# GpSimd computes the factors of a batch's second norm right behind the power of its first

## The chip, the cores and the metric

The kernel runs on one core of a Trainium2 chip, as one launch. The metric is the device time in microseconds (us), lower is better. A comparison uses the median of several runs. The profile is of one further execution, taken by the hardware profiler.

## The reference

One decoder layer over `x` of 16 batches x 256 tokens x 256 features, fp32 throughout. Three sublayers, each added to its input and followed by a layer norm without gain or bias:

```
x = norm(x + recurrent(x))            # projection, causal convolution over 4 tokens, silu,
                                      # a scan over 16 states, projection
x = norm(x + xattn(ctx, latents=x))   # x normed AGAIN inside (rsqrt of its variance, gain, bias),
                                      # q from x, keys/values from 77 context rows and x, 8 heads of 128
x = norm(x + experts(x))              # top 2 of 8 experts, 512 tokens each at most
```

What matters here is the second line: the output of the first norm is normed once more inside the attention. Its mean is 0, so this second norm is a multiplication of each token by one factor, `rsqrt(var * r * r + eps)`, where `var` and `r` are the first norm's variance and reciprocal root.

## The kernel before

**Tiling and stages.** Tokens lie on 128 partitions, so a batch is two tiles of 128 tokens. The main loop runs over 128 heads, 16 batches of 8. For head (b, h) TensorE (PE in the profile) makes keys and queries (`head_kq`: `pk` L609, `pq` L614), then the output of an earlier head (`po` L660), scores (`s` L624) and the transposes of an earlier head's probabilities (`pa`, `pb` L646). ScalarE (ACT) does the exponentials, VectorE (DVE) the maxima (`nm` L626), the reciprocal of the sum (`rs` L632), the division (`p` L634) and a copy of the transposes (`ptt` L648). After the attention the experts follow.

**What is woven in.** Between the heads of batch b the steps that prepare batch b + 1 and finish batch b - 1 are issued, by a table that is written by hand (`steps`, `mid_steps`, `late_steps`: at a given head, ahead of its scores, or behind them). The steps of interest, for a batch nb = b + 1 that is even (b odd):

- head 1: `rec_out(nb)`: the first norm of batch nb. DVE takes mean and variance (L144 to L147), GpSimd (POOL) the power `ra` = (var + eps) ** -0.5 (L136), DVE writes the normed `xs` (L151).
- behind head 1: `scatter_second(b - 3)`, four indirect DMAs that GpSimd issues (L990): rows of two earlier batches go to the experts' lists `xg`. They are held behind `normed[b + 1]`.
- head 2: `project_pairs(b - 1, 0)`: the attention's output projection of batch b - 1, its first three groups of products on PE (`pw`, L750). For it GpSimd adds the residual and the output's bias, `xb = xs + bo` (L743, two instructions), also held behind `normed[b + 1]`.
- head 2: `prep_norm(nb)`: GpSimd computes the factors of the second norm in `again`: `uz` (L159), `u2z` (L161), `u3z` (L163) and the power `rlz` (L136), each on 128x2 values. DVE multiplies `xs` by them: `zl`, two instructions (L522).
- behind head 2: `project_sums(b - 1, 1)`: DVE makes sums of the attention's output for the rest of the projection: `ot` (L729) and `osum` (L730). PE's second part of `pw` at head 3 reads them. Then DVE adds the first part of the projection into `xb` (L764).

For an odd nb, `rec_out(nb)` stands at head 3 of batch b and `prep_norm(nb)` at head 0 of the next batch; there `settle` (factors `uo` to `rlo`, GpSimd's product `o`, L807, and its store to the output on SyncE's queue, SP) and `xb` of another batch stand between the two on GpSimd. Batch 0's are ahead of the loop.

**What sets the order.** Each engine executes its instructions in order. The order on an engine comes from the tile framework's scheduler, which starts from the order in which the program issues instructions and moves them by its own estimates of when each is ready; `tc.issue_after(i)` keeps an instruction from being placed ahead of instruction `i`. `normed[b]` names that instruction: the last power that was recorded (`powers[-1]`) when batch b's first norm was issued.

Of the kernel before, what the change touches and what calls it, by code (L numbers as in the profile page):

```python
# [38 lines left out]
def decoder_layer(  # L39
# [94 lines left out]
    def rsqrt(v, n, rows, name):  # L134
        r = small.tile([P, n], F32, tag="r", name=f"r{name}")
        powers.append(G.tensor_tensor(r[:rows], v[:rows], nhalf[:rows, 0:n], ALU.pow))  # L136
        return r

    def layernorm(dst, src, n, rows, name, behind=None):

        mv = small.tile([P, n, 2], F32, tag="mv", name=f"mv{name}")
        for i in range(n):
            st = small.tile([P, 6], F32, tag="st", name=f"st{name}_{i}")
            V.bn_stats(st[:rows], src[:rows, i, :])  # L144
            V.bn_aggr(mv[:rows, i, :], st[:rows])
        v = small.tile([P, n], F32, tag="v", name=f"v{name}")
        V.tensor_scalar(v[:rows], mv[:rows, :, 1], EPS, None, ALU.add)  # L147
        r = rsqrt(v, n, rows, name)
        for i in range(n):
            with tc.issue_after(behind.ins) if behind is not None else nullcontext():  # L150
                V.tensor_scalar(  # L151
                    dst[:rows, i, 0:D], src[:rows, i, :], mv[:rows, i, 0:1], r[:rows, i : i + 1], ALU.subtract, ALU.mult
                )
        return mv, r

    def again(mv, r, name):

        u = small.tile([P, 2], F32, tag="u", name=f"u{name}")
        G.tensor_tensor(u, mv[:, :, 1], r, ALU.mult)  # L159
        u2 = small.tile([P, 2], F32, tag="u2", name=f"u2{name}")  # L160
        G.tensor_tensor(u2, u, r, ALU.mult)  # L161
        u3 = small.tile([P, 2], F32, tag="u3", name=f"u3{name}")
        G.tensor_scalar(u3, u2, EPS, 1.0, ALU.add, ALU.mult)  # L163
        return rsqrt(u3, 2, P, f"l{name}")
# [40 lines left out]
    def load_x(b):  # L205
        xts[b] = aw.tile([P, 2, D], F32, tag="xt", bufs=3, name=f"xt{b}")
        nc.sync.dma_start(xts[b], x_in[b * S : (b + 1) * S, :].rearrange("(i p) d -> p i d", p=P))
# [116 lines left out]
    sums, yss, xs, stats = {}, {}, {}, {}  # L324
# [90 lines left out]
        for b, r in zip(members, rows):  # L415
            yss[b] = ys[r, :], outw[r, :]

    ysums, normed = {}, {}

    def rec_add(b, n):  # L420

# [12 lines left out]
    def rec_out(b):  # L434

        xs[b] = xpool.tile([P, 2, DX], F32, tag="xs", name=f"xs{b}")
        stats[b] = layernorm(xs[b], ysums.pop(b), 2, P, f"a{b}")
        normed[b] = powers[-1]
        if b + 2 < B:
            load_x(b + 2)  # L440
# [70 lines left out]

    def prep_norm(b):

        r2 = again(*stats.pop(b), f"z{b}")
        zl = b1.tile([P, 2, D], F32, tag="zl", name=f"zl{b}")
        for i in range(2):
            if turned is None:
                V.tensor_scalar(zl[:, i, :], xs[b][:, i, 0:D], r2[:, i : i + 1], None, ALU.mult)
                continue

            with tc.issue_after(turned.ins):
                V.tensor_scalar(zl[:, i, :], xs[b][:, i, 0:D], r2[:, i : i + 1], None, ALU.mult)  # L522
        zs[b] = zl
# [497 lines left out]
    for b in range(B):  # L1021
# [26 lines left out]
        if new_pair:  # L1048
# [3 lines left out]
            elif nb % 4 == 0:  # L1052
                at(b, 0, rec_state, nb, nb + 3)
                amid(b, 0, rec_scan, nb)
            at(b, 1, rec_add, nb, PB)
            at(b, 1, rec_out, nb)
            at(b, 2, prep_norm, nb)
            at(b, 3, rec_out, nb + 1)
            at(b, 3, prep_keys, nb)
            at(b, 3, prep_sums, nb)  # L1060
# [3 lines left out]
        elif b == 0:  # L1064
            for h in range(2):
                at(0, h, rec_in, 0, 2 * h, 1)
                at(0, h, rec_in, 0, 2 * h + 1, 1)
            at(0, 2, load_xT, 1)
            at(0, 2, rec_state, 1, 1)
            amid(0, 2, rec_scan, 1)  # L1070
            at(0, 3, rec_add, 1, 1)
            at(0, 3, rec_out, 1)
            at(0, 4, prep_norm, 1)
            at(0, 4, prep_keys, 1)
            at(0, 4, prep_sums, 1)
            for n, h in enumerate((5, 6, 7)):
                at(0, h, prep_values, 1, n, False)
                behind(0, h, prep_values, 1, n, True)
            for h in range(NCT - FIRST_CTX):
                behind(0, h, context, FIRST_CTX + h, False)  # L1080
        elif nb < B:
            at(b, 0, prep_norm, nb)
            at(b, 0, prep_keys, nb)
            at(b, 0, prep_sums, nb)
            for n, h in enumerate((1, 4, 6)):
                at(b, h, prep_values, nb, n, False)
                behind(b, h, prep_values, nb, n, True)
# [378 lines left out]
```

## Time and profile before

| | us |
|---|---|
| runs | 1169.77, 1172.89, 1169.11 |
| median | 1169.77 |
| the profiled execution | 1171.0 |
| its span, first to last instruction | 1169.3 |
| PE busy | 1135.1 |
| DVE busy | 782.1 |
| ACT busy | 499.0 |
| POOL busy | 316.1 |

Times in rows of the profile are microseconds from the span's start. Busy PE time is that of pipelined matmuls, so neighbouring groups overlap by some 0.2 us. A row that merges several instructions says how many (x4) and gives the time from the first one's start to the last one's end. Tile names have their buffer numbers left out: `ra` is the power of a batch's first norm, `rlz` that of its second, `rb` that of the norm behind the attention, `rlo` that of the last `again`. `A <- B` in a wait means that A's engine stood idle until B was done.

### The profile page before, as it was taken

What the parts mean: (1) busy time and instruction counts of PE and PEld (TensorE: products, weight loads), DVE (VectorE), ACT (ScalarE), POOL (GpSimd) and SP (SyncE); (2) the same over time, 40 slices, a digit from 0 to 9 for tenths busy, and PEclk for the clock granted to TensorE, in tenths of its full rate; (3) what the DMA queues carried; (4) which work ended last, traced back from release to release, by engine and by line L of the source; (5) the groups of instructions that cost most, each with busy time, mean ns of one, the idle gap of its engine ahead of it and who ended that gap; (6) DMA issues with size and microseconds to landing.
All of it is one profiled execution on the core that took longest, in us unless ns stands there. A gap on an engine that the chain in (4) does not pass through costs nothing. (4 is left out here: it accounts for less than half of the span.)

```text
span 1169.3 us, 16020 instructions
## 1 busy us (share of the span) xinstructions
PE 1135.1 (97%) x5380; PEld 821.0 (70%) x5380; DVE 782.1 (67%) x2144; ACT 499.0 (43%) x1315; POOL 316.1 (27%) x565
## 2 busy tenths in 40 slices
PE   7999999999999999999999999999999999999996
PEld 3465676767787777677777777777777778876664
DVE  6655877676657776777567757865567555665666
ACT  3344444453444344444444444444444444523331
POOL 2201241114210530242015302340142014144455
PEclk9999999999999999999999999999999999999998
DMA  8741010001000110010000100000001000046652
GB/s 276 206 128 39 20 38 18 11 28 58 19 12 10 54 36 12 28 40 19 12 10 27 37 11 10 18 19 12 10 17 46 20 10 15 21 159 138 181 160 90
DMA packets 47417, 60.63 MB, mean 52 GB/s; under 512 B 7957, under 2 KB 37374, under 8 KB 47336
## 3 DMA queue, kind: packets, MB, share of 16 engines
q1 hardware_dynamic: 39686, 50.18, 14.1%
q0 software_dynamic: 6048, 9.22, 3.3%
q8 instruction: 42, 0.69, 0.2%
q10 hardware_dynamic: 1602, 0.23, 0.1%
q14 instruction: 39, 0.32, 0.1%
HBM read 36.33 MB, written 30.78 MB: 57 GB/s over the span
## 5 line engine op out<-in xcount | busy, mean ns | idle before, releaser
L660 PE MATMUL po<-ptt,v 128*128 128x256 f32 (+1 forms) x768 | 189.2, 381 | 1.6 <-DVE rs L632 1.6
L660 PEld LDWEIGHTS po<-ptt,v 128*128 128x128 f32 (+1 forms) x768 | 142.0, 190 | 51.7 <-issue 34.4
L609 PE MATMUL pk<-kvt,wkv_s 128*128 128x333 f32 x512 | 165.4, 444 | 0.0
L624 PE MATMUL s<-kt,qt 128*128 128x333 f32 x512 | 164.5, 443 | 0.0
L626 DVE TENSOR_REDUCE nm<-s 128x2 f32<-128x666 f32 x128 | 108.3, 846 | 72.1 <-PE s L624 68.1
L630 ACT ACTIVATE p<-s,nm 128x333 f32<-128x333 f32 x256 | 135.7, 536 | 44.5 <-DVE nm L626 44.2
L614 PE MATMUL pq<-kvt,wq_s 128*128 128x256 f32 x512 | 131.2, 378 | 0.0
L609 PEld LDWEIGHTS pk<-kvt,wkv_s 128*128 128x128 f32 x512 | 91.1, 191 | 45.6 <-issue 22.9
L668 ACT ACTIVATE ot<-po,bkv_s 128x256 f32<-128x256 f32 x128 | 60.9, 476 | 140.3 <-PE po L660 135.7
L624 PEld LDWEIGHTS s<-kt,qt 128*128 128x128 f32 x512 | 96.3, 188 | 31.6 <-issue 1.3
L614 PEld LDWEIGHTS pq<-kvt,wq_s 128*128 128x128 f32 x512 | 96.7, 189 | 30.8 <-issue 1.0
L649 ACT COPY ptt<-pb 77x256 f32<-77x256 f32 x128 | 47.3, 369 | 164.1 <-PE pb L646 161.0
L634 DVE TENSOR_SCALAR p<-p,rs 128x333 f32<-128x333 f32 x256 | 98.5, 421 | 3.3
L990 POOL DMA_INDIRECT xg<-xs,sidx x64 | 66.1, 1032 | 98.3 <-ACT ot L668 38.9
L648 DVE COPY ptt<-pa 128x512 f32<-128x512 f32 x128 | 87.3, 682 | 0.7 <-PE pa L646 0.7
L646 PEld LDWEIGHTS pa<-ident,p 128*128 128x128 f32 x512 | 63.9, 141 | 29.3
L611 ACT ACTIVATE kt<-pk,bkv_s 128x333 f32<-128x333 f32 x128 | 69.1, 540 | 28.2 <-PE pk L609 21.7
L646 PE MATMUL pa<-ident,p 128*128 128x128 f32 x512 | 76.8, 273 | 0.0
L351 DVE SCALAR_TENSOR_TENSOR cv<-hp,cw,cv 128x512 f32<-128x512 f32 (+1 forms) x108 | 74.1, 692 | 1.6
L616 ACT ACTIVATE qt<-pq,bqs 128x256 f32<-128x256 f32 x128 | 61.1, 478 | 20.2 <-PE pq L614 15.3
L336 PE MATMUL ph<-xT,inw 128*128 128x512 f32 (+1 forms) x144 | 63.1, 567 | 5.5 <-DMA inw<-in_in_wT 4.4
L1275 PE MATMUL pf<-w,it 128*128 128x256 f32 x272 | 61.3, 381 | 2.0 <-ACT ye L1285 1.7
(264 smaller groups left out, 1764.6 us busy)
## 6 DMA issues: line engine op xcount, KB each, us to landing
v<-vc SPq DMA_DIRECT2D x16, 308.0 KB
xg<-zero SPq DMA_DIRECT2D x34, 131.0 KB
xe<-xg SPq DMA_DIRECT2D x8, 524.0 KB
xt<-in_x_in SPq DMA_DIRECT2D x16, 256.0 KB
out<-o SPq DMA_DIRECT2D x16, 256.0 KB
w<-in_w1T SPq DMA_DIRECT2D x8, 512.0 KB
w<-in_w2T SPq DMA_DIRECT2D x8, 512.0 KB
oe<-ye SPq DMA_DIRECT2D x15, 256.0 KB
```

Source lines behind the costliest of these rows:

```text
L351: conv = V.scalar_tensor_tensor(cv, hp[:, :, k : k + S], cw[:, c, k : k + 1], cv, ALU.mult, ALU.add)
L609: T.matmul(pk[:, 0:J], lhsT=wkv_s[:, k, f], rhs=kvt[:, k, :], start=(k == 0), stop=(k == DC - 1))
L611: A.activation(kt, pk[:, 0:J], AF.Identity, bias=bkv_s[:, h : h + 1])
L614: T.matmul(pq[:, 0:S], lhsT=wq_s[:, k, f], rhs=kvt[:, k, 0:S], start=(k == 0), stop=(k == DC - 1))
L624: T.matmul(s[:, ic, 0:J], lhsT=qt[:, ic * P : (ic + 1) * P], rhs=kt, start=True, stop=True)
L626: V.tensor_reduce(nm, s[:, :, 0:J], AX.X, ALU.max, negate=True)
L630: A.activation(p[:, ic, :], s[:, ic, 0:J], AF.Exp, bias=nm[:, ic : ic + 1], accum_out=sm[:, ic : ic + 1])
L634: V.tensor_scalar(p[:, ic, :], p[:, ic, :], rs[:, ic : ic + 1], None, ALU.mult)
L646: T.transpose(dst[0:jn, c0 : c0 + P], pn[:, ic, j0 : j0 + jn], ident)
L648: turned = V.tensor_copy(ptt[:, 0:2, :], pt01.rearrange("p (j i) -> p j i", j=2))
L660: T.matmul(po[:, 0:S], lhsT=vs[b][0:jn, jc, h * DH : (h + 1) * DH], rhs=ptt[0:jn, jc, :], start=(jc == 0), stop=(jc == 2),)
L990: dma = G.indirect_dma_start(out=xg[:, :], out_offset=bass.IndirectOffsetOnAxis(ap=sidx[:, t, c : c + 1], axis=0), in_=xs[b + t // GT][:, ...
```

## The change

`again` is called in `rec_out`, directly behind the first norm's `layernorm`, and its result is kept until `prep_norm` fetches it. The instructions themselves are the same. Since the call stands ahead of the line that sets `normed[b]`, the last recorded power is now `rlz` instead of `ra`, and the scatters, `xb` and `settle`, which are held behind `normed`, are held behind `rlz`.

```diff
-    ysums, normed = {}, {}
+    ysums, normed, factors = {}, {}, {}
...
     def rec_out(b):
         xs[b] = xpool.tile([P, 2, DX], F32, tag="xs", name=f"xs{b}")
         stats[b] = layernorm(xs[b], ysums.pop(b), 2, P, f"a{b}")
+
+        factors[b] = again(*stats[b], f"z{b}")
         normed[b] = powers[-1]
         if b + 2 < B:
             load_x(b + 2)
...
     def prep_norm(b):
-        r2 = again(*stats.pop(b), f"z{b}")
+        r2 = factors.pop(b)
         zl = b1.tile([P, 2, D], F32, tag="zl", name=f"zl{b}")
         ...
```

In the built order, on GpSimd, an even batch from 4 on goes from `ra`, 4 scatters, 2 `xb`, `uz`, `u2z`, `u3z`, `rlz` to `ra`, `uz`, `u2z`, `u3z`, `rlz`, 4 scatters, 2 `xb`; an odd batch from `ra` with the factors interleaved among `uo` ... `o` and `xb` to `ra`, `uz`, `u2z`, `u3z`, `rlz` and then these. At batch 1 the factors come ahead of the power `rc` of a context tile.

## The prediction

> **What bounds the kernel now.** First the page: engine shares and the granted clock.
>
> ```profile
> PE 1135.1 (97%) x5380; PEld 821.0 (70%) x5380; DVE 782.1 (67%) x2144; ACT 499.0 (43%) x1315; POOL 316.1 (27%) x565
> PEclk9999999999999999999999999999999999999998
> ```
>
> TensorE (PE) sets the time, at full clock; GpSimd (POOL) is busy for 27% only. So GpSimd matters only where its lateness reaches PE through another engine. The views of who waited for whom (total us, times, longest) show where that happens, first for VectorE (DVE), then for PE:
>
> ```profile
> DVE zl L522 <- POOL rlz L136: 31.7, 6, 5.3
> ```
>
> ```profile
> PE pw L750 <- DVE ot L729: 3.5, 6, 1.3
> PE pw L750 <- DVE ot L726: 1.9, 3, 0.7
> PE po L660 <- DVE rs L632: 1.6, 1, 1.6
> ```
>
> Six times DVE stands some 5.3 us before `zl`, and six times PE stands before a product of `pw` for DVE's `ot` of L729. The timelines say that these are the same six places: the stages that prepare batches 4, 6, 8, 10, 12 and 14. The stage of batch 6, start, duration, instruction, idle time in brackets; GpSimd, DVE, PE:
>
> ```profile
> 393.16 0.72 POOL L136 TENSOR_TENSOR ra<-va,nhalf 128x2 f32<-128x2 f32 x1 [0.67 <-DVE va L147]
> 394.07 1.18 POOL L990 DMA_INDIRECT xg<-xs,sidx  x1 [0.19 <-issue]
> ...
> 399.27 1.33 POOL L743 TENSOR_TENSOR xb<-xs,bo_s 128x256 f32<-128x256 f32 x2
> 400.55 0.20 POOL L159 TENSOR_TENSOR uz<-mva,ra 128x2 f32<-128x2 f32 x1
> ...
> 401.39 0.72 POOL L136 TENSOR_TENSOR rlz<-u3z,nhalf 128x2 f32<-128x2 f32 x1
> ```
>
> ```profile
> 395.76 0.16 DVE L632 RECIPROCAL rs<-sm 128x2 f32<-128x2 f32 x1
> 395.96 0.90 DVE L634 TENSOR_SCALAR p<-p,rs 128x333 f32<-128x333 f32 x2
> 402.14 0.61 DVE L522 TENSOR_SCALAR zl<-xs,rlz 128x256 f32<-128x256 f32 x2 [5.29 <-POOL rlz L136]
> 402.68 0.68 DVE L729 TENSOR_TENSOR ot<-osum,ot 128x512 f32<-128x512 f32 x1
> 404.07 0.61 DVE L764 TENSOR_TENSOR xb<-xb,u 128x128 f32<-128x128 f32 x2
> 405.36 0.68 DVE L648 COPY ptt<-pa 128x512 f32<-128x512 f32 x1
> ```
>
> ```profile
> 399.32 0.60 PE L646 MATMUL pa<-ident,p 128*128 128x128 f32 x4
> 401.10 1.02 PE L614 MATMUL pq<-kvt,wq_s 128*128 128x256 f32 x4
> 403.41 1.16 PE L750 MATMUL pw<-wosum,ot 128*128 128x128 f32 x8 [1.29 <-DVE ot L729]
> 404.41 1.06 PE L750 MATMUL pw<-wo_s,ot 128*128 128x128 f32 x8
> 407.53 1.46 PE L660 MATMUL po<-ptt,v 128*128 128x256 f32 x6
> ```
>
> GpSimd has `ra` at 393.88, but runs four scatters (5.2 us) and the two `xb` additions (1.3 us) before the factors. `rlz` ends at 402.11, `zl` starts at 402.14, `ot` (L729) behind it, and PE waits. In the seven odd stages, whose `zl` stands two heads earlier, it is the reverse: DVE waits for PE before L729 (6.0 us in 7) and PE never waits there.
>
> **The change part by part.** Nothing is added or removed; four GpSimd instructions (`uz`, `u2z`, `u3z`, `rlz`) move up for each of fifteen batches, and what they pass moves back. In the built order, PE's and ScalarE's instructions stand as before. On DVE, in the same six stages, the first half of `zl` comes ahead of the two divisions `p` (L634). On SP six stores of `o` fall behind a load.
>
> (1) Even stages 4 to 14. The four instructions take 401.39+0.72-400.55 = 1.56 us, 1.6 with the hand-over. So `rlz` ends at 393.88+1.6 = 395.5, where DVE's turn at `zl` comes at 395.96 (stage of batch 4: `ra` ends 276.12, so 277.7 against 278.2). Then `zl`, `p`, `p`, `zl` and L729 run through: `ot` is written by 395.96+0.90+0.61+0.68 = 398.2, and PE needs it at 401.10+0.87 = 401.97 (0.87 is the step from `pq` to the next group without a stall, as 276.70 to 277.57). The stall goes with 3.8 us in hand. Its price: PE's idle time at the six places is 0.19, 1.29, 0.17, 1.29, 0.19 and 0.40, in sum 3.53 us. A stall costs more than its idle time: from `pq` to `pw` PE took 2.31 us instead of 0.87, and the next step 1.00 instead of 0.89, so 1.55 for 1.29 idle; in the stage of batch 4 it is 0.45 for 0.19. That is 0.26 on each. Gain 3.53 + 6 x 0.26 = 5.1 us; bounds 3.5 (idle alone) and 5.1.
>
> (2) What comes late next. The scatters and `xb` move back by 1.6 us, and DVE needs `xb` at L764: this is the new wait. In the stage of batch 6 the scatters then start at 395.7, end at 400.9, and `xb` at 402.2; DVE, through with L730 at about 399, stands idle some 3 us. Queued behind L764 are `nm` of the next head and `ptt`, for which PE's `po` waits. L764 now starts at 402.3 instead of 404.07, so `ptt` is written by 404.2; `po`, 1.55 earlier, wants it at 405.98. Slack 1.8 us (2.8 in the other four stages). Cost 0. Once `xb` slips by more than that slack, each further us is PE's.
>
> (3) Where `zl` stands ahead of `p`: `p` ends 0.35 us later (397.2), and PE turns it (`pa`) at 399.32. Hidden by 2.1 us here, by 3.2 in the stage of batch 4.
>
> (4) Batch 1. `rc` of a context tile stands between `u2z` and `u3z` now (86.97) and comes behind `rlz`: it ends at about 88.7 instead of 87.64. Its reader on DVE (ctx, L151) ran at 88.50, and PE waited for that at 88.97. So 0.2 us lost; bounds 0 and 1.1 (the whole delay).
>
> (5) Batch 3. PE stood 1.63 us at 170.90 for DVE. There DVE's pair at L151 took 1.30 us beside GpSimd's `xb`, against 0.74 at 164.33 without it, and L351 1.12 against 0.74: `xb` costs DVE up to 0.9 us. It now starts 1.6 later and falls beside other DVE work. Bounds: 0.9 gained and 0.4 lost; I take 0.3 gained, about the middle.
>
> (6) The rest at nothing. Batch 2: `xb` also moves past L151 (1.46 instead of 0.74) but stays ahead of the L726 that PE waits for at 149.98: bounds 0.7 either way. Odd batches from 5: `rlz` earlier, `xb` and `o` at most 1.6 later, first read of `xb` some 40 us on (296.98 to 338.06). Scatters: `xg` is read only at the end. SP's stores: they go behind loads issued in 0.4 us, and `o` is overwritten a batch (60 us) later.
>
> Sum: -5.1 + 0.2 - 0.3 = -5.2 us. The profiled execution took 1171.0 us (span 1169.3), so 1165.8; the median of the three runs lies 1.2 lower, 1169.77, so 1164.6.
>
> **A rule against it.** The move takes GpSimd's work out of DVE's idle gap and puts it beside DVE's work. The trace has rows for that: the first two scatters, beside L151, L648, L726 and `p` (3 us of DVE), took 1.18 and 1.14 us, the later two, beside an idle DVE, 0.98; and factors beside L151 and `ptt` at batch 1 kept their 0.20, 0.20, 0.19 and 0.70. So 0.4 us of slip, inside the slack. The Trainium skill, SBUF — State Buffer, section "Who interferes with whom", says that a VectorE instruction in a two-port mode and a GpSimd instruction lock each other out for a whole instruction, not in part, and its section on the two sides adds that descriptors of GpSimd's own DMAs wait likewise. What full blocking would give is the first rival.
>
> **The rivals.** (a) GpSimd is shut out while DVE works. Price: scatters would stand still for `p`, `zl`, L729 and L730, 0.90+0.61+0.68+0.69 = 2.9 us, then DVE itself stops at L764. `xb` slips 2.9: 1.1 beyond the slack in the stages of batches 6 and 10, 0.1 in four, so 2.6 us of the 5.2 are lost: 1167.2, no measurable difference. For it: L151 at 1.30 beside `xb`. Against: the scatter rows above. 13%.
>
> (b) The wait for `rlz` stays, and now `p` stands behind half of `zl`. It decides once `rlz` comes over 2.1 us (batches 6, 10) or 3.2 us (the others) after DVE's turn, then 1:1. The factors' slowest row, 144.61 to 147.22, is 2.6 us, only 1.0 more than taken, which speaks against it. If `rlz` came as late as now (402.11), `p` would end at 403.4, 4.1 us behind PE's need, and 3.0 in the other four: 20 us with no gain, 1190. Half of that gives 1180; slower. 7%.
>
> (c) The factors come early but PE meets the next limit: `ptt` or `kvt` is late by what was gained, as all engines lose the time the stalls gave them. Against it stand the odd stages, which run without stall. Gain 0 to 2, about 1169. 8%.
>
> (d) The moved `xb` helps DVE more (batches 2 and 3, all of 0.9 and 0.7): gain 6.5, 1163.3. 6%.
>
> **How the numbers follow.** Forecast 66%, with (d) 72% faster by over 0.3% (3.5 us, about what a measurement of this kernel can tell from no change); (a) and (c) 21% within; (b) 7% slower. Range: from (d) with a little scatter, 1163.0, to (a) plus 1.0 for the runs' own spread, 1168.2; it leaves out (b) and (c), 15%, and takes in the bounds of (4) and (5) one at a time.
>
> **What would show it.** Right: DVE's wait for `rlz` at L522 gone (under 3 us in all); a new wait of DVE at L764 for `xb`, some 2 to 3.5 us in six stages; no PE wait for `ot` L729; PE's other waits as they were, that of `ctx` up by 0.2. Wrong: PE waiting for `p`, `ptt` or `rs` in the six stages, scatters far over 1.2 us, or `rlz` over 2.5 us behind `ra`.

## The result

| | before | after |
|---|---|---|
| median of 20 runs, us | 1171.04 | 1165.38 |
| lowest to highest | 1168.13 to 1173.54 | 1162.91 to 1170.47 |
| ratio after / before | | 0.9949, 95% interval 0.9941 to 0.9958 |
| span of the profiled execution | 1169.3 | 1162.6 |

The change makes the kernel faster, by 6.0 us by the ratio (4.9 to 6.9) and 5.7 by the medians; 5.2 was forecast. The forecast of 1164.6 us started from three runs of before; from the median of 20 runs, 5.2 us less would be 1165.8.

The line numbers of after are those of before plus two from `prep_norm` on: L729 is L731 now, L764 is L766. The views of who waited for whom (us in total, times, longest), DVE first, then PE:

```profile
DVE xb L766 <- POOL xb L745: 21.0, 6, 3.5
```

```profile
PE pt L468 <- DVE ctx L151: 3.3, 3, 1.6
PE pw L752 <- DVE ot L728: 2.1, 3, 0.9
PE po L662 <- DVE rs L634: 1.2, 1, 1.2
```

DVE's 31.7 us of waiting for `rlz` are gone, and 21.0 us for `xb` have come in the same six stages. PE's 3.5 us before the second part of `pw` are gone, and no new wait of PE has come in these stages. PE's three waits for `ctx` grew from 2.4 to 3.3 us, but only 0.13 us of that is the wait at batch 1; the other two stand ahead of the loop, near 12 and 19 us, where GpSimd's order is that of before. The stage of batch 6 in the timelines of after; GpSimd, DVE, PE:

```profile
392.89 0.72 POOL L136 TENSOR_TENSOR ra<-va,nhalf 128x2 f32<-128x2 f32 x1 [0.67 <-DVE va L147]
...
394.52 0.69 POOL L136 TENSOR_TENSOR rlz<-u3z,nhalf 128x2 f32<-128x2 f32 x1
395.38 1.12 POOL L992 DMA_INDIRECT xg<-xs,sidx  x1 [0.17 <-issue]
...
400.45 1.34 POOL L745 TENSOR_TENSOR xb<-xs,bo_s 128x256 f32<-128x256 f32 x2
```

```profile
395.57 0.34 DVE L524 TENSOR_SCALAR zl<-xs,rlz 128x256 f32<-128x256 f32 x1
395.82 0.84 DVE L636 TENSOR_SCALAR p<-p,rs 128x333 f32<-128x333 f32 x2
...
396.83 0.70 DVE L731 TENSOR_TENSOR ot<-osum,ot 128x512 f32<-128x512 f32 x1
401.83 0.62 DVE L766 TENSOR_TENSOR xb<-xb,u 128x128 f32<-128x128 f32 x2 [3.51 <-POOL xb L745]
...
403.13 0.68 DVE L650 COPY ptt<-pa 128x512 f32<-128x512 f32 x1
```

```profile
399.05 0.60 PE L648 MATMUL pa<-ident,p 128*128 128x128 f32 x4
401.69 1.05 PE L752 MATMUL pw<-wosum,ot 128*128 128x128 f32 x8
405.70 1.46 PE L662 MATMUL po<-ptt,v 128*128 128x256 f32 x6
```

`rlz` ends at 395.21, ahead of DVE's turn; `ot` is written by 397.53, 4.2 us before PE asks for it at 401.69, and PE goes through `pw` at its usual 0.89 us a group. DVE stands 3.5 us for `xb`, and `ptt` is still written by 403.81, 1.9 us before PE's `po`.

Where the time went is seen best by how far the same PE group starts earlier or later in the two timelines:

| PE group | before | after | shift |
|---|---|---|---|
| `pt` of a context tile, batch 1 | 88.97 | 89.38 | +0.41 (+0.28 stood there at 83.25 already) |
| `po` behind batch 2's stage | 150.98 | 151.58 | +0.60 |
| `po` in batch 3's stage | 170.90 | 171.08 | +0.18 |
| `po` behind batch 4's stage | 289.77 | 289.49 | -0.28 |
| `po` behind batch 6's stage | 407.53 | 405.70 | -1.83 |
| `pc` (L941) of batches 8, 9 | 744.21 | 740.41 | -3.80 |
| first `pe`, experts | 1048.95 | 1043.92 | -5.03 |

From batch 3 to the experts this is 5.2 us, and it comes in steps at the even stages. The two profiled executions differ by 0.28 at the start and by another 1.7 in the experts, where before had one wait of 1.50 us at 1082.85 (`pf` for `ye`); the run of the second experiment, which has before's order there, had none of that size. Those are differences of single executions, and the medians do not need them.

### The profile page after: what moved, and what is told of

Its sections match the earlier page's. It is cut to its first block, busy times and chain, and to the rows that moved or that the text cites. A ratio compares the mean times of both kernels' runs of the same rounds, so it can differ in the third digit from the quotient of the medians.

```text
span 1162.6 us, 16038 instructions
## 1 busy us (share of the span) xinstructions
PE 1133.2 (97%) x5380; PEld 822.2 (71%) x5380; DVE 777.6 (67%) x2144; ACT 499.0 (43%) x1315; POOL 315.7 (27%) x565
## 4 chain that ended last, share of the span: by engine, by line
PE 82%; DVE 11%; DMA 3%; issue 1%; POOL 1%; ACT 1%; POOLq 0%; SPq 0%; DVEq 0%; ACTq 0%
PE po L662 12%; PE s L626 11%; PE pk L611 10%; PE pq L616 8%; PE pv L576 8%; PE pw L752 7%; PE pi L1250 4%; PE pa L648 4%; PE pf L1277 4%; PE ph L336 4%; DVE cv L351 2%; PE pb L648 2%; PE pvc L494 2%; PE pw L680 1%; DVE nm L628 1%
## 5 line engine op out<-in xcount | busy, mean ns | idle before, releaser
L351 DVE SCALAR_TENSOR_TENSOR cv<-hp,cw,cv 128x512 f32<-128x512 f32 (+1 forms) x108 | 74.6, 697 | 1.6
L1250 PE MATMUL pi<-xet,w 128*128 128x512 f32 (+1 forms) x144 | 61.5, 574 | 1.6 <-issue 1.6
```

Of the source, the lines that this page charges most:

```text
L351: conv = V.scalar_tensor_tensor(cv, hp[:, :, k : k + S], cw[:, c, k : k + 1], cv, ALU.mult, ALU.add)
L1250: T.matmul(pi[:, 0:c], lhsT=w1[:, k, f * P : (f + 1) * P], rhs=xet[:, k, 0:c], start=(k == 0), stop=(k == DC - 1),)
```

## The experiments

Each was timed against the kernel before in runs of its own chip, so each has its own median of before. The theory: PE's stall before the second part of `pw` in the six even stages was the whole gain, it is a threshold, and the wait for `xb` lies within slack. The rivals: GpSimd's work beside DVE's (the port), or a gain in proportion to how early the factors come.

| run | this, us | before, us | difference | ratio, 95% interval |
|---|---|---|---|---|
| e1, even stages alone | 1162.36 | 1167.90 | -5.5 | 0.9952 (0.9939 to 0.9966) |
| e2, all the others alone | 1166.85 | 1167.90 | -1.1 | 0.9993 (0.9984 to 1.0002) |
| e3, behind the scatters | 1183.41 | 1167.90 | +15.5 | 1.0144 (1.0128 to 1.0159) |
| e3b, the same, `p` first | 1164.79 | 1167.90 | -3.1 | 0.9979 (0.9970 to 0.9988) |
| e4, 1.3 us more ahead | 1179.16 | 1167.62 | +11.5 | 1.0098 (1.0083 to 1.0112) |
| e5, `xb` ahead of scatters | 1162.41 | 1167.62 | -5.2 | 0.9955 (0.9944 to 0.9967) |
| e6, `xb` 4 us later | 1180.56 | 1167.62 | +12.9 | 1.0114 (1.0099 to 1.0128) |
| e7, sums before the norm | 1160.85 | 1167.62 | -6.8 | 0.9942 (0.9929 to 0.9955) |
| e8, behind two scatters, `p` first | 1162.34 | 1168.05 | -5.7 | 0.9947 (0.9934 to 0.9961) |
| e9, after again | 1162.15 | 1168.05 | -5.9 | 0.9953 (0.9940 to 0.9967) |
| e10, e7 again | 1161.19 | 1168.05 | -6.9 | 0.9943 (0.9930 to 0.9957) |

### Which batches: e1 and e2

```diff
-        factors[b] = again(*stats[b], f"z{b}")
+        if b >= 4 and b % 2 == 0:          # e2: if not (b >= 4 and b % 2 == 0)
+            factors[b] = again(*stats[b], f"z{b}")
         normed[b] = powers[-1]
...
-        r2 = factors.pop(b)
+        r2 = factors.pop(b) if b in factors else again(*stats[b], f"z{b}")
```

> The factors are early in the six even stages (batches 4 to 14) alone; batches 1, 2, 3 and the odd ones keep the order of before. Theory (the gain is the PE stall before L729 in the six even stages): -5.1 us against the kernel before, nearly the whole gain; PE's wait for ot at L729 gone. Rival (the gain comes from GpSimd's xb no longer lying beside DVE's L151, in the odd stages and at batches 2 and 3): under -1 us.

> The complement: factors early for batches 1, 2, 3 and the odd ones, late as before in the six even stages. Theory: 0 us within 0.5 against the kernel before (batch 1 costs some 0.15, batch 2 some 0.2, batch 3 gains some 0.4, by PE's shifts in the trace of after); the six stalls before L729 stay, 3.5 us idle in sum. Rival (xb beside L151): -4 to -6 us.

The even stages alone give -5.5 us, the others nothing that is clear of zero. In e2 the stall stands as it was (who waited for whom, PE; L732 is L729 of before):

```profile
PE pw L753 <- DVE ot L732: 3.5, 6, 1.3
```

So the gain comes from these six stages, and `xb` lying beside L151 elsewhere, which should have given 4 to 6 us in e2, is not it. By the ratio e2 gained 0.8 us (from 1.9 gained to 0.2 lost), so whether the other batches gain nothing or about 1 us is left open by its time; PE's shifts in the table above put them near nothing.

### How early is early enough: e3, e3b, e8

In the six even stages `again` is issued behind `scatter_second`; e3b holds `zl` behind the divisions `p` as well; e8 puts two scatters ahead and two behind.

```diff
 # in rec_out
-        factors[b] = again(*stats[b], f"z{b}")
         normed[b] = powers[-1]
+        if not (b >= 4 and b % 2 == 0):
+            factors[b] = again(*stats[b], f"z{b}")
+            normed[b] = powers[-1]
...
 # in scatter_second; e8: last = the scatters of range(GT, GT + 1), normed = those of the rest, behind the factors
         with tc.issue_after(normed[b + 4].ins):
-            scatter(b, sidxs[b], range(GT, 2 * GT))
+            last = scatter(b, sidxs[b], range(GT, 2 * GT))
+        with tc.issue_after(last.ins):
+            factors[b + 4] = again(*stats[b + 4], f"z{b + 4}")
+        normed[b + 4] = powers[-1]
...
 # in prep_norm, e3b and e8 alone; divided holds the divisions p
-            with tc.issue_after(turned.ins):
+            with tc.issue_after((divided[-1] if b >= 4 and b % 2 == 0 else turned).ins):
                 V.tensor_scalar(zl[:, i, :], xs[b][:, i, 0:D], r2[:, i : i + 1], None, ALU.mult)
```

> In the six even stages the factors stand behind the four scatters and ahead of xb only: rlz comes 1.3 us earlier than before instead of 6.6. DVE's order is that of after, with the first half of zl ahead of the divisions p. Theory: L729 is no longer late, but p now waits for rlz, and PE for p: 2.7 + 0.3 us in each of two stages, 1.6 + 0.3 in four, so 13.8 lost and 5.1 regained, +8.5 us against before. Rival (what counts is how early the factors are, in proportion: 1.3 of 6.6): -1 us.

> As the run with the factors behind the scatters, but zl is held behind the divisions p, so that DVE's order is that of the kernel before. Theory: zl and L729 come 1.3 us earlier than before, at 402.0 in the stage of batch 6, where PE wants ot at 401.97; the stall is gone but for 0 to 0.3 us in two stages: -4.5 us, from -3.8 to -5.2. Rival (in proportion): -1 us. Rival (the port: scatters ahead or behind matter): between.

> In the six even stages two scatters, the factors, two scatters, xb; zl held behind p, as in the run before it (p first). Theory (a threshold): rlz comes at about 398.3 in the stage of batch 6, ot is written by 399.6, and PE wants it at 401.97, so all of the gain is there: -5.2 us against before, though rlz is 2.8 us later than in after; and zl no longer lies beside xb, so L522's pair takes 0.6 us. Rival (in proportion: 3.9 of the 6.6 us by which after is earlier): -3 us.

**e3** is slower, as the theory said and the proportional rival did not, but by 15.5 us, not 8.5. PE's wait is where it was expected (2 x 2.7 + 4 x 1.6 = 11.8 us of idle time worked out, 13.5 found), and 10 of the 15.5 are that less the 3.5 it replaces. The rest shows in the stretches of the timeline: length, busy us of PE, PEld, DVE, ACT and POOL (with the number of instructions), the granted clock of PE, DMA share, GB/s. First the waits, then three stretches behind the stall of batch 4's stage (PE starts again at 283.80) and one behind that of batch 6's (405.03):

```profile
PE pa L650 <- DVE p L638: 13.5, 6, 3.0
```

```profile
283.00:285.00 2.00, 1.20 (x7) 1.04 (x8) 1.91 (x5) 0.00 (x0) 0.55 (x1) 0.88 0.00 0
285.00:287.00 2.00, 2.00 (x5) 1.23 (x5) 1.96 (x5) 0.37 (x1) 0.00 (x0) 0.50 0.00 0
287.00:289.00 2.00, 2.00 (x11) 1.68 (x10) 1.35 (x4) 1.95 (x6) 0.00 (x0) 0.77 0.00 0
...
405.00:407.00 2.00, 1.97 (x10) 1.51 (x11) 1.90 (x5) 0.37 (x1) 0.00 (x0) 1.00 0.00 0
```

Behind three of the six stalls (of 1.86, 1.85 and 1.84 us) the granted clock fell to 0.50 for some 3.4 us, and the groups of that time took longer: at 529.77 the four groups from `pa` to `pq` took 4.58 us, against 2.89 at 405.03, behind a stall at full clock. That is 1.7 us more; at 283.80 and 775.78 it is 1.7 and 1.6. In sum these are 5.0 us, and 10 + 5.0 comes close to the 15.5 measured.

**e3b** keeps DVE's order of before. It gains 3.1 us by the medians, 2.5 by the ratio (1.4 to 3.5), under the 3.8 to 5.2 expected and over the 1 of the rival. The stall is gone in four stages; in two 0.86 us of it are left. DVE, GpSimd and PE in the stage of batch 6:

```profile
400.45 1.46 DVE L527 TENSOR_SCALAR zl<-xs,rlz 128x256 f32<-128x256 f32 x2 [4.01 <-POOL rlz L136]
```

```profile
400.39 1.36 POOL L748 TENSOR_TENSOR xb<-xs,bo_s 128x256 f32<-128x256 f32 x2
```

```profile
402.56 1.16 PE L755 MATMUL pw<-wosum,ot 128*128 128x128 f32 x8 [0.86 <-DVE ot L734]
```

`zl` came 1.3 us earlier than before, as it should, but then lay beside `xb` and took 1.46 us instead of 0.61; the 0.85 us are what is left of the stall. In the Trainium skill, SBUF — State Buffer, section "Who interferes with whom", a VectorE instruction in a two-port mode and a GpSimd instruction shut each other out. For this pair the trace agrees on one side only: `zl` lost 0.85 us, while `xb` took 1.36 us, as without a neighbour (1.33 before); in which mode `zl` ran, the trace does not show.

**e8** tests the threshold without that meeting: `rlz` comes 2.8 us later than in after (it ends at 398.32), DVE waits for it again, and the time is that of after (-5.7 beside -5.9 for e9, timed on the same chip). The waits of DVE, and DVE and PE in the stage of batch 6:

```profile
DVE xb L769 <- POOL xb L748: 13.4, 6, 2.2
DVE zl L527 <- POOL rlz L136: 8.8, 6, 1.5
```

```profile
398.36 0.61 DVE L527 TENSOR_SCALAR zl<-xs,rlz 128x256 f32<-128x256 f32 x2 [1.48 <-POOL rlz L136]
401.99 1.05 PE L755 MATMUL pw<-wosum,ot 128*128 128x128 f32 x8
```

`zl` takes its 0.61 us, PE does not stand before `pw`, and the proportional rival's 3 us lie outside the interval. 8.8 us of DVE's waiting cost nothing; only what reaches `ot` too late for PE counts.

### The slope beyond the threshold: e4

Two `xb`-like additions into a tile that nobody reads, behind `xb` and ahead of the factors, in the order of before.

```diff
-        r2 = again(*stats.pop(b), f"z{b}")
+        if b >= 4 and b % 2 == 0:
+            with tc.issue_after(xb_last[b - 2].ins):
+                for j in range(2):
+                    late = G.tensor_tensor(idle, xs[b - 2][:, j, 0:D], bo_s, ALU.add)
+            with tc.issue_after(late.ins):
+                r2 = again(*stats.pop(b), f"z{b}")
+        else:
+            r2 = again(*stats.pop(b), f"z{b}")
```

> The order of the kernel before, with two more GpSimd additions of 128x256 (1.3 us, their result is read by nobody) ahead of the factors in the six even stages. Theory: PE already waits there for L729, so each us comes through 1:1: 6 x 1.33 = +8 us against before. Rival (DVE's wait is mostly covered, PE waits by chance): 0 to +2 us.

PE's waits and a stretch behind the stall of batch 6's stage:

```profile
PE pw L757 <- DVE ot L736: 11.8, 6, 2.7
```

```profile
406.00:408.00 2.00, 1.47 (x7) 1.47 (x8) 1.86 (x5) 0.00 (x0) 0.00 (x0) 0.50 0.00 0
```

The idle time grew by 11.8 - 3.5 = 8.3 us, the 8 of the theory. The other 3 of the 11.5 us are two stalls of 2.68 us, around whose end the clock fell (at 406.53 the groups of `pw` took 1.3 us more, at 651.34 1.6); behind the four of 1.56 to 1.78 us it did not.

### The new wait: e5 and e6

```diff
 # e5: in project_pairs, part 0; scatter_second is no longer called on its own
             for j in range(2):
-                G.tensor_tensor(xb[:, j, :], xs[b][:, j, 0:D], bo_s, ALU.add)
+                xb_last[b] = G.tensor_tensor(xb[:, j, :], xs[b][:, j, 0:D], bo_s, ALU.add)
+            if b - 2 in sidxs:
+                with tc.issue_after(xb_last[b].ins):
+                    scatter(b - 2, sidxs[b - 2], range(GT, 2 * GT))
...
 # e6: ahead of the same two additions, which are held behind `held`
+            held = normed[b + 2]
+            if b >= 2 and b % 2 == 0:
+                with tc.issue_after(scattered[b - 2].ins):
+                    for j in range(6):
+                        held = G.tensor_tensor(idle, xs[b][:, j % 2, 0:D], bo_s, ALU.add)
```

> As after, but in the six even stages xb stands ahead of the scatters, right behind the factors. Theory: DVE's new wait for xb (21.0 us in after) all but vanishes, nm and ptt come 3 us earlier, and the time stays that of after, -5.2 us against before, since PE had 1.9 us and more in hand there. Rival (DVE's 21 us of waiting cost PE something): -6.5 to -9 us. Rival (xb beside p and L729 slows them): up to +1 us against after.

> As after, with six more GpSimd additions (4.0 us, read by nobody) between scatters and xb in the six even stages. Theory: slack from ptt to PE's po is 1.9 us in the stages of batches 6 and 10 and 3.0 in the other four, so 2.1 and 1.0 us are lost, and some 0.26 each for the stall: 9.8 us, so +4.5 us against before (3.0 without the 0.26). Rival (no slack): 24 lost, +18. Rival (xb is not on PE's path): -5.

In e5 DVE's wait for `xb` is gone from the list and the time is that of after: the 21.0 us cost nothing. `xb` beside DVE did slow DVE there (in the stage of batch 6 the first half of `zl` took 0.74 us instead of 0.34, `p` 1.11 instead of 0.84), and that was hidden too. In e6 the wait grows to 47.7 us and PE pays, for `ptt`, as it was said:

```profile
PE po L662 <- DVE ptt L650: 12.4, 10, 2.5
```

The size was wrong: +12.9 us, not +4.5. `xb` came 4.5 us later, so the stalls were 2.54 and 1.44 instead of 2.1 and 1.0; four stages stalled again at the next head (0.34 each), which the expectation had left out; and the clock fell behind both stalls of 2.5 us. 12.4 - 3.5 = 8.9 of idle time and two falls of about 1.7 make 12.3.

### A further step: e7, e9, e10

The three waits of PE for `ot` that are left in after (L728, 2.1 us) come ahead of the factors: DVE does two L151 first. `rec_out` of an even batch is issued behind `project_sums`:

```diff
 behind(b, 1, project_sums, b - 1, 0)
+if nb % PB == 0:
+    behind(b, 1, rec_out, nb)
...
-            at(b, 1, rec_out, nb)
```

> As after, but rec_out of an even batch is issued behind project_sums, so that on DVE ot (L728 in after) comes ahead of the two L151 in the six even stages. PE waited there for it in the stages of batches 6 and 10, 0.62 and 0.61 us. Theory: these two stalls go, 0.62 + 0.26 each: -1.7 us against after, -7 against before; rlz is later by nothing, as ra does not move. Rival (p, now behind half of L151, or zl, both halves behind p, come late): 0 or slower than after.

> The changed kernel again, unaltered, on the same chip and beside the same runs of the kernel before as the next one: -5.2 to -6.0 us.

> The version with the sums ahead of the norm's L151 again, beside the changed kernel itself: 1.7 us less than that (two stalls of 0.6 idle and 0.26 behind it). If the difference is under 0.5 us, the two stalls gone in the trace are given back elsewhere.

In the stages of batches 6 and 10 the stall is gone. The third group of `pw`, after and then e7:

```profile
395.63 1.16 PE L752 MATMUL pw<-wo_s,ot 128*128 128x128 f32 x8 [0.62 <-DVE ot L728]
```

```profile
394.85 1.12 PE L752 MATMUL pw<-wo_s,ot 128*128 128x128 f32 x8
```

`rlz` came 0.6 us later there than in after (`u3z` took 0.57 us and the power 0.92, beside `ot`, L151 and `p`), which the expectation had put at nothing, and DVE's wait for `xb` grew from 21.0 to 25.6 us; neither reached PE. The median stands 1.0 us under that of after (e10 beside e9, timed on the same chip), with intervals that overlap; the profiled spans 1.9 (1159.6 beside 1161.5). It is the fastest version measured, and the two stalls of 0.6 are shown to go; that it beats after by the 1.7 us worked out is not settled.

## Why the prediction was right

- **The six stalls (5.1 us).** Right in place and size: 5.2 us by the shifts of PE's groups, in steps of 0.46 at batch 4 and 1.55 at batch 6, where 0.45 and 1.55 were worked out. That 0.26 us a stall on top of its idle time belong to the price shows here: idle time alone would have made 3.5. e1, e2 and e4 show the place, e8 that it is a threshold.
- **The new wait for `xb`.** 3.5 us in six stages, where some 3 were expected, with a slack of 1.9 us at batch 6, where 1.8 was worked out. e5: it costs nothing. e6: it would, once the slack is used up.
- **`zl` ahead of `p`.** Hidden, as said. e3 is rival (b) made real: in the stage of batch 6 `rlz` came 4.9 us after DVE's turn, and PE waited 2.94 us for `p`, about the 4.9 - 2.1 of the rival's rule.
- **Batch 1.** 0.13 us lost (0.2 said). **Batch 3.** The stall of 1.63 became 1.20, 0.4 gained (0.3 said): both L151 took 0.74, but L351, beside `xb` now, 1.26. **Batch 2**, put at nothing within 0.7, lost 0.2 (PE's stall of 0.69 became 0.89).
- **The rule against it**, rival (a). The scatters took 1.12, 0.97, 1.09 and 0.98 us and the factors 0.20, 0.19, 0.19 and 0.69: 0.3 us of slip in each of the six stages, no shutting out there. e3b shows a pair that does collide, `zl` beside `xb`, which the change keeps apart.
- **Rival (c)**, the next limit taking the gain, was not seen. **Rival (d)**: the time does not separate 5.2 from its 6.5 us, since the interval, 4.9 to 6.9, holds both; PE's shifts do, with 0.2 lost at batch 2 and 0.4 gained at batch 3 where (d) had 0.7 and 0.9 gained.

What was mis-sized was not in the prediction but in the expectations: the price of a longer PE stall, which has a second term, the clock (e3, e4, e6).

## What to carry to other kernels

An engine that is idle for most of the time can still hold the busiest one: follow the wait from engine to engine to its head, and look what stands in front of that instruction in its queue. Price a stall of the busiest engine by the start-to-start time of its groups, not by its idle time alone; moving the late value earlier by just that much is enough, as e8 shows. Here 31.7 us of a second engine's waiting had cost 5.2 us of the kernel's time, while the 21.0 us that came instead cost nothing. When a scheduler sees a value become early, it moves its readers too: check what now stands behind them, since they become the path if the value is late after all.

## What the runs showed of the hardware

The granted clock can halve around a PE stall of about 1.8 to 2.7 us: it read 0.50 for some 3.4 us, from late in the stall or just behind it, at three stalls of 1.84 to 1.86 us in e3, two of 2.54 and 2.55 in e6 and two of 2.68 in e4, at about 1.3 to 1.7 us of further loss each. In the attention, stalls up to 1.78 us left it at 1.00, but so did stalls of 2.07, 2.94 and 2.95 us in e3, so length alone does not decide. The Trainium skill, TensorE: Matmul & The Clock Gate, Part 1, has the clock fall after at least one idle window of some 3.4 us; the shorter stalls here disagree with that as a lower bound. The Trainium skill, in the same Part 1, has that window run free, whatever the kernel does; that would fit that the length alone does not decide, which no run here tests.

Two further prices, each for a pair of DVE instructions beside the two GpSimd additions `xb`: `zl` 1.46 us instead of 0.61 (e3b), L151 1.46 instead of 0.74 (before, batch 2). In the stage of batch 2 of after both sides lost: `xb` took 1.89 us there, while DVE's `osum` took 1.22 instead of 0.68 and an L351 1.12 instead of 0.75.
